# Two layers of a channel-wise likelihood as 32x32 products in differing array tiles

## The chip, the cores and the metric

The kernel runs on one core of one Trainium2 chip. The metric is the device time of one execution in microseconds (us). Before the change the median of three runs was 16118.02 us (16114.57 to 16145.0). A profile holds the engine records and the granted TensorE clock of one execution.

## The reference

A clustered attention and an MLP with a depthwise 3x3 convolution come first. The change lies in what follows, a likelihood for each of 192 channels. Each channel has its own four tiny layers (1 to 3, 3 to 3, 3 to 3, 3 to 1), applied to x - 0.5 and to x + 0.5, which I call the two sides:

```python
def _logits_cumulative(x, Ms, bs, fs):
    for i, (M, b) in enumerate(zip(Ms, bs)):
        x = jnp.einsum('coi,cin->con', jax.nn.softplus(M), x) + b
        if i < len(fs):
            x = x + jnp.tanh(fs[i]) * jnp.tanh(x)
    return x
...
lower = _logits_cumulative(flat - 0.5, Ms, bs, fs)
upper = _logits_cumulative(flat + 0.5, Ms, bs, fs)
s = jax.lax.stop_gradient(-jnp.sign(lower + upper))
pmf = jnp.abs(jax.nn.sigmoid(s * upper) - jax.nn.sigmoid(s * lower))
...
return jnp.maximum(pmf, LIKELIHOOD_BOUND)
```

There are 4 images of 128 x 128 tokens. A block is 512 tokens, so there are 128 blocks, 32 for each image.

## The kernel before

Forty channels make a group, with 3 filters 120 rows; the last of the five groups has 32 channels. A layer of a group is one product with a 120x120 block-diagonal matrix for each side. The convolution's taps are VectorE instructions, and the scheduler puts them between VectorE's instructions for the likelihood of another block.

```python
def bend(g, layer, src):                      # src + gate * tanh(src + bias)
    m = rows_of(g)
    t = pool.tile([R, 2, NB], F32, tag="t", bufs=2, ...)
    for s in range(2):
        nc.scalar.activation(t[:m, s, :], src[:m, s, :], AF.Tanh, bias=bias[:m, layer, g, s:s + 1])
    u = pool.tile([R, 2, NB], F32, tag="u", bufs=6, ...)
    nc.vector.scalar_tensor_tensor(u[:m], t[:m], gate[:m, layer, g:g + 1], src[:m], ALU.mult, ALU.add)
    return u
...
for layer, lw in ((1, l1w), (2, l2w)):
    for g in range(NG):
        m = rows_of(g)
        ps = ps2(f"h{layer}_{n}_{g}")         # one of two PSUM tiles of two banks
        for s in range(2):
            mm(ps[:m, s, :], lhsT=lw[:m, g].rearrange("p c o -> p (c o)")[:, :m],
               rhs=us[g][:m, s, :], start=True, stop=True)
        us[g] = bend(g, layer, ps)
for part, b3t, c0, m, gs in ((l3a, bias3a, 0, CA, (0, 1, 2)), (l3b, bias3b, CA, CB, (3, 4))):
    ps = ps2(f"h3_{n}_{m}")
    ...                                       # layer 3: products l3a, then l3b
    nc.vector.tensor_tensor(lu[:m], lu[:m], sg[:m]...., ALU.mult)
...
# convolve(i): the taps, on VectorE
nc.vector.scalar_tensor_tensor(
    acc[:, k, r0:r1, :], src[:, k, s0:s0 + r1 - r0, dx:dx + W],
    dwt[:, k, t:t + 1], acc[:, k, r0:r1, :], ALU.mult, ALU.add)
...
for i in range(NBLK + 2):
    ...                                       # expand(i): norm, transposes, fc1
    convolve(i - 1)
    likelihood(i - 2)
```

Of the kernel before, what the change touches and what calls it, by code (L numbers as in the profile page):

```python
# [9 lines left out]
F32 = mybir.dt.float32  # L10
# [9 lines left out]
C = 192          # channels  # L20
C1 = C - P       # channels in the second chunk of a contraction
HEADS = 8
D = C // HEADS   # 24
M = 64           # cluster means
MLP = 384
W = 128          # image width: 128 tokens are one image row
NB = 512         # tokens in a block
NJ = NB // P     # token tiles (= image rows) in a block
G = 40           # channels in a group of the last layer
CA = 3 * G       # channels of part a of the last layer, three groups  # L30
CB = C - CA      # channels of part b, two groups
R = 3 * G        # rows (channel, filter) of a group
NG = 5
HR = 32          # rows or columns of a head: 24, and some for its shifts or its sum
# [5 lines left out]
def conv_seq_kernel(  # L40
# [7 lines left out]
    NT = N // P      # token tiles, attention groups, image rows  # L48
# [18 lines left out]
    # ---------------------------------------------------------------- constants  # L67
# [6 lines left out]
    # tri[k, m] = 1 where k < m  # L74
# [9 lines left out]
    # cluster numbers less M, all negative, and each token's own number  # L84
# [7 lines left out]
    # ---------------------------------------------------------------- weights  # L92
    # Contractions over the channels are in two chunks, of 128 and of 64 rows. Where a
    # layer norm comes before, its gain scales the rows, and a 65th row of the second
    # chunk, against ones, holds what its offset contributes.
# [18 lines left out]
    l0a = const([CA, 3, G, 3], "l0a")  # L114
    l0b = const([CB, 2, G, 3], "l0b")
    l1w = const([R, NG, G, 3], "l1w")
    l2w = const([R, NG, G, 3], "l2w")
    l3a = const([R, 3, CA], "l3a")
    l3b = const([R, 2, CB], "l3b")
    gate = const([R, 3, NG], "gate")  # L120
    bias = const([R, 3, NG, 2], "bias")
# [3 lines left out]
    def rows_of(g):  # L125
        return R if g < NG - 1 else 3 * (C - (NG - 1) * G)

    with tc.tile_pool(name="prep", bufs=2) as prep:
# [8 lines left out]
        def norm_params(g, b, name):  # L137
            ga, gb = load(g, 1, f"g_{name}", 1)
            # the offset as a 65th column, so that its product lands on partition 64
# [31 lines left out]
        # A head has 32 rows: 24 of its own, one for each of the two shifts of a query's  # L171
        # scores (against its keys and against the means), and 6 zeros. Keys have a one
        # in the first of the two, the means' keys in the second.
# [4 lines left out]
        # and values a one, for the sum of a query's weights  # L178
# [3 lines left out]
        # the means: unit vectors to compare with, keys and values  # L182
# [53 lines left out]
        # Wproj @ Wconv  # L236
# [17 lines left out]
        # The last layer's matrices: softplus(m) = max(m, 0) + log1p(exp(-|m|)), in columns  # L254
        # by rows (channel, filter) of a group, and by channels for its first layer.
        NS = 8 * NG + 6
        raw = prep.tile([P, NS], F32, bufs=1)
        nc.vector.memset(raw, 0.0)
        rawg = raw[:, 0:8 * NG].rearrange("p (g e) -> p g e", e=8)
        vecs = prep.tile([R, 6, NG], F32, bufs=1)  # L260
        nc.vector.memset(vecs, 0.0)
        m0r = m0.rearrange("c (o u) -> (c o) u", u=1)
        for g in range(NG):
            n = rows_of(g)
            s = slice(g * R, g * R + n)
            nc.sync.dma_start(out=rawg[:n, g, 0:1], in_=m0r[s, :])
            nc.sync.dma_start(out=rawg[:n, g, 1:4], in_=m1[s, :])
            nc.sync.dma_start(out=rawg[:n, g, 4:7], in_=m2[s, :])
            nc.sync.dma_start(out=rawg[:n, g, 7:8], in_=m3[s, :])
            for e, v in enumerate((b0, b1, b2, f0, f1, f2)):  # L270
                nc.sync.dma_start(out=vecs[:n, e, g:g + 1], in_=v[s, :])
        nc.sync.dma_start(out=raw[:CA, 8 * NG:8 * NG + 3], in_=m0[0:CA, :])
        nc.sync.dma_start(out=raw[:CB, 8 * NG + 3:NS], in_=m0[CA:C, :])
        sp = prep.tile([P, NS], F32, bufs=1)
        e1 = prep.tile([P, NS], F32, bufs=1)
        u1 = prep.tile([P, NS], F32, bufs=1)
        c1 = prep.tile([P, NS], F32, bufs=1)
# [3 lines left out]
        # log1p(e) = log(u) + (e - (u - 1)) / u with u the rounded 1 + e  # L281
# [8 lines left out]
        spg = sp[:, 0:8 * NG].rearrange("p (g e) -> p g e", e=8)  # L290
        nc.scalar.activation(gate, vecs[:, 3:6, :], AF.Tanh)

        # rows (c, i) against columns (c', o): one where c = c'
        mask = prep.tile([R, G, 3], F32, bufs=1)
        nc.vector.memset(mask, 1.0)
        nc.gpsimd.affine_select(out=mask, in_=mask, pattern=[[-3, G], [0, 3]], base=0,
                                channel_multiplier=1, compare_op=ALU.is_ge, fill=0.0)
        nc.gpsimd.affine_select(out=mask, in_=mask, pattern=[[3, G], [0, 3]], base=2,
                                channel_multiplier=-1, compare_op=ALU.is_ge, fill=0.0)
# [593 lines left out]
```

## Time and profile before

| | before |
|---|---|
| median of the runs | 16118.02 us |
| span of the profiled execution | 16111.9 us |
| mean granted TensorE clock | 0.883 |
| layers 1 and 2 on TensorE (L786) | 2397.7 us busy |
| one block, mean of 116, from one layer 1 to the next (29 for each image; its last blocks run alone and are shorter) | 63.71 us |

In a row of the costliest groups stand the line, engine and operation, what is written from what, the shapes, the count, the busy time with the mean of one, and the idle time of that engine ahead of it with what ended it. PE stands for TensorE, PEld for its weight loads, DVE for VectorE, ACT for ScalarE and POOL for GpSimd. In a timeline a line has the start, the duration, the engine, the operation and, in brackets, the idle time of the engine ahead of it. The prediction shows these views of the kernel before.

### The profile page before, as it was taken

To read this page: it belongs to the slowest core of one execution; us is meant where nothing else is said; L and a number is where in the kernel's file an instruction comes from. 1 tells how busy PE (TensorE), PEld (TensorE's weight loads), DVE (VectorE), ACT (ScalarE), POOL (GpSimd) and SP (SyncE) were. 2 spreads that over 40 slices of the span, in tenths; PEclk is the share of its full clock that TensorE was granted. 3 is DMA by queue.
4 is the path that set the end of the run, shared out by engine and by line. 5 is a ranking of instruction groups with operands and counts; after the bars stand their busy time and mean duration, and the time that the engine had idled before them with its cause. 6 is when DMAs were issued, how large, how long until landed. Compare 5 with 4: busy or idle time off the path is not lost.

```text
span 16111.9 us, 185400 instructions
## 1 busy us (share of the span) xinstructions
PE 13647.8 (85%) x72162; PEld 7179.5 (45%) x72162; DVE 9317.3 (58%) x16584; ACT 6563.8 (41%) x9595; POOL 3769.5 (23%) x4503
## 2 busy tenths in 40 slices
PE   6669998888877999788887799988888999988888
PEld 5546663333354666333335466533333566533333
DVE  6534446777753444677776344477777344477776
ACT  1023334555512333455551233355555333355555
POOL 1441112222214111222211411122222211122222
PEclk6579998999967999899995899989999999999999
DMA  2100000000020000000002000000000000000000
GB/s 72 58 14 19 17 16 26 19 19 19 13 65 14 19 19 15 26 18 20 19 13 65 16 17 19 18 22 20 19 18 13 19 17 19 22 20 18 20 19 12
DMA packets 297421, 366.60 MB, mean 23 GB/s; under 512 B 56479, under 2 KB 206431, under 8 KB 296543
## 3 DMA queue, kind: packets, MB, share of 16 engines
q1 hardware_dynamic: 231006, 253.71, 5.3%
q0 software_dynamic: 65536, 101.02, 2.4%
q8 instruction: 570, 9.34, 0.2%
q14 instruction: 309, 2.52, 0.1%
HBM read 203.31 MB, written 151.26 MB: 22 GB/s over the span
## 4 chain that ended last, share of the span: by engine, by line
PE 53%; DVE 23%; issue 8%; POOL 7%; ACT 6%; DMA 2%; SPq 0%; POOLq 0%; DVEq 0%; ACTq 0%
DVE acc_f L741 8%; PE st L597 7%; DVE u_f L772 6%; PE h_f L786 4%; PE av L622 4%; PE h_f L794 4%; PE sm L560 4%; DVE mx L561 4%; PE ph_f L718 3%; PE ps_a L522 3%; PE ps_a L523 3%; PE ph_f L719 2%; PE av L625 2%; ACT t_f L770 2%; POOL sg_f L800 2%
## 5 line engine op out<-in xcount | busy, mean ns | idle before, releaser
L770 ACT ACTIVATE t_f<-h_f,bias 120x512 f32<-120x512 f32 (+1 forms) x3840 | 2394.7, 683 | 1714.9 <-PE h_f L786 1313.2
L741 DVE SCALAR_TENSOR_TENSOR acc_f<-hd_f,dwt,acc_f 128x128 f32<-128x128 f32 (+2 forms) x5304 | 2500.3, 517 | 565.0 <-ACT hd_f L720 514.9
L772 DVE SCALAR_TENSOR_TENSOR u_f<-t_f,gate,h_f 120x1024 f32<-120x1024 f32 (+1 forms) x1920 | 2416.0, 1274 | 243.6 <-ACT t_f L770 240.7
L600 ACT ACTIVATE es<-st 128x1024 f32<-128x1024 f32 (+1 forms) x1024 | 1043.1, 1020 | 2387.9 <-PE st L597 2335.2
L597 PE MATMUL st<-qa,kt_a 26*128 26x256 f32 (+1 forms) x8192 | 1163.1, 410 | 364.1 <-DVE mx L561 364.1
L786 PE MATMUL h_f<-u_f,l2w 120*120 120x512 f32 (+1 forms) x2560 | 1204.5, 606 | 247.4 <-DVE u_f L772 247.3
L561 DVE TENSOR_REDUCE mx<-sm 128x4 f32<-128x1024 f32 (+1 forms) x1024 | 1202.4, 1217 | 336.3 <-PE sm L560 193.3
L786 PE MATMUL h_f<-u_f,l1w 120*120 120x512 f32 (+1 forms) x2560 | 1193.2, 605 | 28.6 <-DVE u_f L772 28.6
L688 POOL DMA_INDIRECT at_f<-at_d,pos x512 | 616.9, 1205 | 2149.7 <-PE pb_gf L383 1901.2
L645 POOL TENSOR_TENSOR ot<-on 128x192 f32<-128x192 f32 x512 | 302.9, 592 | 3331.7 <-DVE on L641 3330.2
L597 PEld LDWEIGHTS st<-qa,kt_a 26*128 26x128 f32 x8192 | 707.3, 190 | 814.7 <-DVE mx L561 757.8
L534 DVE COPY va_a<-pv_a 128x512 f32<-128x512 f32 x256 | 177.0, 691 | 1410.2 <-PE pv_a L533 1410.2
L802 DVE TENSOR_TENSOR lu_f<-lu_f,sg_f 120x1024 f32<-120x1024 f32 (+1 forms) x256 | 317.3, 1240 | 1080.8 <-ACT sg_f L801 1080.7
L718 PE MATMUL ph_f<-ta_f,fc 128*128 128x512 f32 x768 | 607.0, 883 | 394.9 <-ACT ta_f L381 394.9
L800 POOL TENSOR_TENSOR sg_f<-lu_f 120x512 f32<-120x512 f32 (+1 forms) x256 | 383.3, 1497 | 2187.0 <-ACT lu_f L798 2177.4
L786 PEld LDWEIGHTS h_f<-u_f,l2w 120*120 120x120 f32 (+1 forms) x2560 | 417.4, 178 | 1011.7 <-DVE u_f L772 627.0
L794 PE MATMUL h_f<-u_f,l3a 120*120 120x512 f32 x1536 | 692.1, 600 | 128.1 <-DVE u_f L772 128.1
L786 PEld LDWEIGHTS h_f<-u_f,l1w 120*120 120x120 f32 (+1 forms) x2560 | 441.4, 180 | 746.5 <-issue 602.2
L622 PE MATMUL av<-es,va_a 128*32 128x128 f32 x16384 | 769.6, 307 | 0.0
L639 DVE RECIPROCAL rec<-ao 128x16 f32<-128x16 f32 x512 | 131.7, 257 | 1098.4 <-PE ao L636 1098.4
L629 ACT COPY sums<-av 128x512 f32<-128x512 f32 x512 | 299.8, 585 | 1110.8 <-PE av L625 1099.8
L579 DVE TENSOR_TENSOR qa<-qt_a,pm 128x256 f32<-128x256 f32 x512 | 215.5, 421 | 894.9 <-PE pm L578 893.0
(291 smaller groups left out, 23682.5 us busy)
## 6 DMA issues: line engine op xcount, KB each, us to landing
xn_d<-xn_c SPq DMA_DIRECT2D x128, 384.0 KB
at_d<-ot SPq DMA_DIRECT2D x128, 384.0 KB
xa_c<-in_x SPq DMA_DIRECT2D x128, 256.0 KB
xa_f<-in_x SPq DMA_DIRECT2D x128, 240.0 KB
out<-pm_f SPq DMA_DIRECT2D x128, 240.0 KB
xb_f<-in_x SPq DMA_DIRECT2D x128, 144.0 KB
out<-pm_f SPq DMA_DIRECT2D x128, 144.0 KB
xb_c<-in_x SPq DMA_DIRECT2D x128, 128.0 KB
```

Of the source, the lines that this page charges most:

```text
L560: mm(psv[:, h, t, 0:n], lhsT=qt[r, t, qs], rhs=kt[r, t, c0:c0 + n], start=True, stop=True)
L561: nc.vector.tensor_reduce(mx[:, :, 2 * a:2 * a + 2, D].rearrange("p t h -> p h t"), psv[:, :, :, 0:n], AX.X, ALU.max)
L597: mm(psv[:, h, t, :], lhsT=kt[r, t, ks], rhs=qa[r, t, q0_:, :].rearrange("p w q -> p (w q)"), start=True, stop=True)
L600: nc.scalar.activation(e[:, :, :, q0_ * P:], psv, AF.Exp)
L622: mm(av[HR * r:HR * r + HR, 0, t, :], lhsT=blocks[k // NJ][2][:, k % NJ, 4 * t + r, :], rhs=es[r // 2][:, r % 2, t, c0:c0 + P], start=w == ...
L718: mm(ps, lhsT=fc1_0[:, s], rhs=ta, start=True, stop=False)
L741: nc.vector.scalar_tensor_tensor(acc[:, k, r0:r1, :], src[:, k, s0:s0 + r1 - r0, dx:dx + W], dwt[:, k, t:t + 1], acc[:, k, r0:r1, :], ALU. ...
L770: nc.scalar.activation(t[:m, s, :], src[:m, s, :], AF.Tanh, bias=bias[:m, layer, g, s:s + 1])
L772: nc.vector.scalar_tensor_tensor(u[:m], t[:m], gate[:m, layer, g:g + 1], src[:m], ALU.mult, ALU.add)
L786: mm(ps[:m, s, :], lhsT=lw[:m, g].rearrange("p c o -> p (c o)")[:, :m], rhs=us[g][:m, s, :], start=True, stop=True)
L794: mm(ps[:m, s, :], lhsT=part[:r, k], rhs=us[g][:r, s, :], start=k == 0, stop=k == len(gs) - 1)
L800: nc.gpsimd.tensor_tensor(sg[:m], lu[:m, 0, :], lu[:m, 1, :], ALU.add)
```

## The change

The intent: in a 120x120 block-diagonal product only one cell in forty does anything. Ten channels (30 rows, padded to 32) are enough for a product of their own, and eight such products (four quarters, two sides) lie in eight different 32x32 tiles of the array, meant to run at the same time. In layer 1 a quarter's output is turned to other rows, by a step that differs with the side, so that the sides' tiles differ as well. As the two sides then have their gates in different rows, layer 1's u_f is made side by side.

```diff
+    def turn(layer, g, s):
+        return 2 * (g % 2) + s if layer == 1 else 0
...
-                    nc.vector.scalar_tensor_tensor(u[:m], t[:m], gate[:m, layer, g:g + 1], src[:m], ALU.mult, ALU.add)
+                    for v in ([slice(0, 1), slice(1, 2)] if layer == 1 else [slice(0, 2)]):
+                        nc.vector.scalar_tensor_tensor(u[:, v], t[:, v], gate[:, layer, g, v.start:v.start + 1],
+                                                       src[:, v], ALU.mult, ALU.add)
...
-                        for s in range(2):
-                            mm(ps[:m, s, :], lhsT=lw[:m, g].rearrange("p c o -> p (c o)")[:, :m],
-                               rhs=us[g][:m, s, :], start=True, stop=True)
+                        for q in range(Q):
+                            for s in range(2):
+                                r = 32 * ((q + turn(layer - 1, g, s)) % Q)
+                                c = 32 * ((q + turn(layer, g, s)) % Q)
+                                w = l1w[r:r + 32, g] if layer == 1 else l2w[r:r + 32, g, s]
+                                mm(ps[c:c + 32, s, :], lhsT=w, rhs=us[g][r:r + 32, s, :], start=True, stop=True)
```

Cut from the diff: the preparation of weights, gates and biases in the new rows, layers 0 and 3 on 128 rows or columns, and comments.

## The prediction

> **What bounds the kernel now.** I read the busy shares and slices first, then the costliest groups, then the timeline of one block, then the busy time of short windows with the granted clock. The page:
>
> ```profile
> PE 13647.8 (85%) x72162; PEld 7179.5 (45%) x72162; DVE 9317.3 (58%) x16584; ACT 6563.8 (41%) x9595; POOL 3769.5 (23%) x4503
> ...
> PEclk6579998999967999899995899989999999999999
> ...
> L770 ACT ACTIVATE t_f<-h_f,bias 120x512 f32<-120x512 f32 (+1 forms) x3840 | 2394.7, 683 | 1714.9 <-PE h_f L786 1313.2
> ...
> L772 DVE SCALAR_TENSOR_TENSOR u_f<-t_f,gate,h_f 120x1024 f32<-120x1024 f32 (+1 forms) x1920 | 2416.0, 1274 | 243.6 <-ACT t_f L770 240.7
> ...
> L786 PE MATMUL h_f<-u_f,l2w 120*120 120x512 f32 (+1 forms) x2560 | 1204.5, 606 | 247.4 <-DVE u_f L772 247.3
> ...
> L786 PE MATMUL h_f<-u_f,l1w 120*120 120x512 f32 (+1 forms) x2560 | 1193.2, 605 | 28.6 <-DVE u_f L772 28.6
> ```
>
> The two L786 rows are what changes: 2397.8 us of TensorE, 15% of the span. PE at 85% suggests a big prize, but that is an average. The MLP and likelihood stage has 4 x 32 = 128 blocks; from 2700 to 4300 us a block takes 63.7 us (mean of 24 starts of the same instruction), half of the whole time. Inside a block, layers 1 and 2 are a ring: TensorE makes h_f in one of two PSUM tiles, ScalarE makes t_f, VectorE makes u_f and so frees the tile. The TensorE and VectorE timelines of layer 2 of one block:
>
> ```profile
> 3313.12 3.71 PE L786 MATMUL h_f<-u_f,l2w 120*120 120x512 f32 x8 [0.94 <-DVE u_f L772]
> 3317.89 3.81 PE L786 MATMUL h_f<-u_f,l2w 120*120 120x512 f32 x8 [1.05 <-DVE u_f L772]
> 3322.77 5.41 PE L794 MATMUL h_f<-u_f,l3a 120*120 120x512 f32 x12 [1.07 <-DVE u_f L772]
> ```
>
> ```profile
> 3314.71 1.93 DVE L741 SCALAR_TENSOR_TENSOR acc_f<-hd_f,dwt,acc_f 128x128 f32<-128x128 f32 x4
> 3316.56 1.27 DVE L772 SCALAR_TENSOR_TENSOR u_f<-t_f,gate,h_f 120x1024 f32<-120x1024 f32 x1
> 3317.75 0.75 DVE L741 SCALAR_TENSOR_TENSOR acc_f<-hd_f,dwt,acc_f 128x512 f32<-128x512 f32 x1
> 3318.41 1.27 DVE L772 SCALAR_TENSOR_TENSOR u_f<-t_f,gate,h_f 120x1024 f32<-120x1024 f32 x1
> 3319.60 1.92 DVE L741 SCALAR_TENSOR_TENSOR acc_f<-hd_f,dwt,acc_f 128x384 f32<-128x384 f32 x3
> ```
>
> TensorE does two groups per 4.8 us and is busy 3.7 of them, but VectorE has almost no holes: its queue fills the ring with convolution taps. Averaged over the 24 blocks, VectorE idles only 0.22, 0.44, 0.28 and three times 0.04 us between the first u_f of layer 0 and the u_f of group 3 in layer 2: 1.05 us of 27.9. So the stretch is **bound by VectorE's queue and the ring at nearly the same length**. VectorE's large holes (7.2 us before the first L802 of a block, 3.7 before the first tap on the new hd_f, 1.5 for the norm) are in the stretches that follow, behind layer 3 and behind the transposes and fc1 products, which the change leaves alone.
>
> [...] L622 (128-row, 32-column tiles, 128 columns streamed, f32) runs 16 records in 0.66 us, in sets of four started 13 to 14 ns apart, one set per 109 ns; one after the other they would take 16 x 107 ns = 1.7 us. The step to the next mode is 203 ns from the last start.
>
> ```profile
> 1523.73 0.66 PE L622 MATMUL av<-es,va_a 128*32 128x128 f32 x16
> 1524.33 0.44 PE L625 MATMUL av<-eg,vgx 128*64 128x128 f32 x4
> ```
>
> [...] Here four row tiles write one bank, in different partitions; no trace of before shows that case. [...] (PEclk column, 1.00 or 0.50):
>
> ```profile
> 3327.76:3331.18 3.42, 3.42 (x9) 1.14 (x8) 0.00 (x0) 1.58 (x3) 1.26 (x1) 1.00 0.00 0
> 3331.18:3334.59 3.41, 1.10 (x10) 0.68 (x7) 2.64 (x9) 3.22 (x4) 0.25 (x2) 1.00 0.00 0
> 3334.59:3338.00 3.41, 1.81 (x8) 1.18 (x8) 1.63 (x4) 0.69 (x2) 3.32 (x3) 0.50 0.00 0
> ...
> 3344.83:3348.24 3.41, 3.41 (x5) 1.33 (x4) 2.09 (x5) 1.31 (x2) 1.37 (x1) 0.50 0.04 11
> 3348.24:3351.65 3.41, 3.41 (x9) 1.48 (x8) 2.42 (x8) 2.64 (x5) 0.00 (x0) 1.00 0.11 32
> ```
>
> [...] After an idle stretch the fc1 products need 4 to 7 us to get full clock back.
>
> **The change, part by part.**
> 1. TensorE, layers 1 and 2. A 120x120 product of 512 columns is two records 429 ns apart; a group has two sides, so 4 x 0.429 = 1.72 us. After, a group is 8 products in 8 different tiles, two per row group and two per column group. If they overlap as L622's do, a group streams 2 x 0.429 us plus 7 x 13.5 ns of starts = 0.95 us. For 10 groups: 17.2 to 9.5 us a block, so 128 x 7.7 = **986 us of TensorE time go**, most of it off the path.
> 2. The ring. Its 4.76 us (load at 3313.12 to load at 3317.88) are: 1.39 to the last record's start, 0.63 until ScalarE starts, 1.42 for the two tanh and hand-over, 1.27 for u_f, 0.05. The first term becomes about 0.63, so the ring 4.0 us for two groups. VectorE needs 9.3 us of work for the four groups of layer 2 that took 9.65, so VectorE becomes the sole bound.
> 3. VectorE. Layer 1's u_f is split by side: 2 x 0.66 for 1.19 us (start to start), +0.13 x 5 = 0.65 us a block. The order listing puts one 0.53 us tap behind group 3 instead of before it. With 0.13 us plus columns/0.96 ns per instruction, which fits the starts in the trace, the work from u_f of layer 0 to group 3 of layer 2 is 26.42 before and 26.54 us after; measured were 27.87. So at most 1.3 us a block, and of the named idle 1.05 - 0.12 = **0.9 us a block, 120 us in all, if the clock stays full**.
> 4. The clock. In layer 2 a row group now streams 0.87 us per group of about 2.3 us, 0.38: [...] I expect half clock by the second half of layer 2. Then a group takes 1.9 us, the ring 5.0, and layer 2 is bound by it: the gain shrinks to about 0.5 us. Then layer 3 starts cold. Its 12 records take 5.15 us on the chain to VectorE's 7.2 us hole; TensorE idles some 1 us before them, [...] **+2.15 us**. Sum with half clock: -0.5 + 2.15 = +1.6 us a block, x 128 = about +200 us.
> 5. Preparation: about 100 small copies more at the start, at some 0.1 to 0.2 us, beside loads: under 20 us. Layers 0 and 3 use 128 rows or columns for 120: free, since time goes by the columns streamed. ScalarE's 683 ns stay.
>
> **The rivals.**
> A. Full clock stays [...]: -120 us, 16000. B. Half clock from layer 2 into layer 3: +200, 16320. C. The tiles don't overlap [...]: 8 products in two waves are as long as before; in four waves a group takes 3.4 us and layers 1 and 2 are bound by TensorE, +15 us a block, far slower. For overlap: L622's four column tiles, and pairs of L597's row tiles starting 6 ns apart. Against: four row tiles in one bank are new. D. TensorE really is the bound, and 986 us come off: against it stand VectorE's full queue, and that of the 276.0 us of idle ahead of these products (247.4 + 28.6), 275.9 ended with VectorE's u_f.
>
> **Range and chances.** A 0.3, B 0.6, C 0.1 (at about +600 as a mean of mild and bad): 0.3 x (-120) + 0.6 x 200 + 0.1 x 600 = +144 us, so 16260. The low end is A with all 1.3 us recovered (-165 gives 15950); the high end is B with 6 us until full clock in every block (3 us lost: +320) and layer 1 partly cold too, 16500. Faster by 2% would need 2.5 us a block, more than VectorE's idle in the stretch: 0.03. Slower by 2% needs +2.5 us a block: B at its worst or C, 0.16.
>
> **What would show it.** Step 1: L786's successor busy near 1200 us for both layers, starts of 8 records within 0.1 us. Steps 2 and 3: VectorE's idle before u_f well under 243.6 us, DVE busy up by about 80 us. Step 4: mean granted clock under 0.883, PEclk below 9 in the slices of this stage, and l3a's 12 records longer than 5.4 us. If the clock stays and the time falls, A; if l3a stays at 5.4 us while the time rises, the half-clock story is wrong. A much longer L786 is C.

The terms of the sum: -0.5 + 2.15, given as +1.6 us a block or about +200 us, and with the chances +144 us, 16260. Two of its steps are estimates. The first is that 0.38 of a window's time (1.30 of 3.41 us) brings half clock; the views show a window at full clock with 1.10 us of work in 3.41 that was followed by half clock, and one at half clock with 3.41 us that was followed by full. The second is the +2.15 us: layer 3a at half clock for 4.3 us in the mean, half of them lost. In the trace of before records of 512 columns that follow each other start 429 ns apart at full clock and 853 ns at half (medians), and in all 120 places where the fc1 products begin anew, full clock came 3.65 to 6.99 us after their first start. For the other estimates of the prediction the same trace has: VectorE's instructions of 128, 384, 512 and 1024 columns, one after the other, start 0.26, 0.53, 0.66 and 1.19 us apart; TensorE's records of 512 columns have a median duration of 592 or 593 ns with 72x120, 120x120 and 128x120 alike (rows x columns); small copies in the preparation (128x64) start 0.13 us apart.

## More of the kernel before

The instruction that multiplies lu_f by its sign runs once a block for the first 120 channels, so the distance between its starts is the time of a block. From VectorE's timeline of the kernel before:

```profile
2694.04 1.23 DVE L802 TENSOR_TENSOR lu_f<-lu_f,sg_f 120x1024 f32<-120x1024 f32 x1 [7.22 <-ACT sg_f L801]
...
2757.89 1.22 DVE L802 TENSOR_TENSOR lu_f<-lu_f,sg_f 120x1024 f32<-120x1024 f32 x1 [7.22 <-ACT sg_f L801]
...
2822.23 1.23 DVE L802 TENSOR_TENSOR lu_f<-lu_f,sg_f 120x1024 f32<-120x1024 f32 x1 [7.22 <-ACT sg_f L801]
...
2885.14 1.23 DVE L802 TENSOR_TENSOR lu_f<-lu_f,sg_f 120x1024 f32<-120x1024 f32 x1 [7.22 <-ACT sg_f L801]
```

The blocks take 63.85, 64.34 and 62.91 us, together 191.10, and then the same three come again. The instructions are the same in each.

## The result, and the profile after

| | before | after |
|---|---|---|
| runs in the same rounds, us | 16112.38 to 16145.0, median 16116.3 | 16156.76, 16181.08, 16200.82, 16230.05; median 16190.95 |
| span of the profiled execution, us | 16111.9 | 16154.7 |
| mean granted clock | 0.883 | 0.845 |

The ratio is 1.0043 (95% interval 1.0025 to 1.0061). A ratio here and below is the mean time of one kernel's fast runs over the mean of the other's in the same rounds, so it is not quite the ratio of the medians quoted. The time is the same within 2%, as expected, but it rose by about half of the 142 us that were predicted. The executions of the changed kernel also spread over 73 us, more than twice as far as before.

The page of the changed kernel: the engines, the granted clock in 40 slices, and the rows of u_f, layer 2, layer 3a and layer 1.

```profile
PE 13107.1 (81%) x87582; PEld 6649.4 (41%) x87582; DVE 9394.2 (58%) x17398; ACT 6553.2 (41%) x9595; POOL 3667.6 (23%) x4495
...
PEclk6579998888867999888885799988888999988888
...
L807 DVE SCALAR_TENSOR_TENSOR u_f<-t_f,gate,h_f 128x1024 f32<-128x1024 f32 (+1 forms) x2560 | 2484.6, 1007 | 129.9 <-ACT t_f L803 120.8
...
L824 PE MATMUL h_f<-u_f,l2w 32*32 32x512 f32 x10240 | 950.3, 809 | 473.0 <-DVE u_f L807 469.0
...
L830 PE MATMUL h_f<-u_f,l3a 128*120 128x512 f32 x1536 | 775.8, 660 | 203.8 <-DVE u_f L807 203.8
...
L824 PE MATMUL h_f<-u_f,l1w 32*32 32x512 f32 x10240 | 616.6, 706 | 130.0 <-DVE u_f L807 124.3
```

Layers 1 and 2 now keep TensorE busy for 950.3 + 616.6 = 1566.9 us instead of 2397.7. VectorE waits half as long ahead of u_f (129.9 for 243.6 us), and its busy time is 77 us higher. Digits of 8 have come into the clock's row, and layer 3a takes 84 us more. Its mean hides what happens. TensorE's timeline has these four blocks in a row:

```profile
3151.31 7.11 PE L830 MATMUL h_f<-u_f,l3a 128*120 128x512 f32 x12 [2.07 <-DVE u_f L807]
...
3215.20 5.41 PE L830 MATMUL h_f<-u_f,l3a 128*120 128x512 f32 x12 [1.30 <-DVE u_f L807]
...
3277.67 7.11 PE L830 MATMUL h_f<-u_f,l3a 128*120 128x512 f32 x12 [2.07 <-DVE u_f L807]
...
3341.57 5.41 PE L830 MATMUL h_f<-u_f,l3a 128*120 128x512 f32 x12 [1.35 <-DVE u_f L807]
```

Layer 3a either has its old duration or is 1.70 us longer. Two stretches say why. They are cut at the edges of the clock's windows, which the trace's clock records place on a fixed grid (3.4133 us in the mean over the trace, and no record off it by more than 0.001). A row gives the stretch, its length, the busy time of PE, PEld, DVE, ACT and POOL with counts, then the granted clock (rounding at the cut makes 0.97 of 1.00 and 0.53 of 0.50). First the end of layer 2 and layer 3a of the block whose products start at 3215.20:

```profile
3203.63:3207.04 3.41, 1.09 (x16) 0.21 (x16) 3.41 (x6) 1.39 (x4) 0.00 (x0) 0.97 0.16 48
3207.04:3210.45 3.41, 2.29 (x24) 0.45 (x32) 3.41 (x7) 2.22 (x4) 0.14 (x1) 0.50 0.00 0
3210.45:3213.87 3.42, 3.42 (x32) 0.23 (x16) 3.35 (x6) 1.48 (x3) 0.00 (x0) 0.53 0.00 0
3213.87:3217.28 3.41, 2.11 (x12) 1.02 (x6) 3.00 (x4) 1.26 (x2) 0.00 (x0) 1.00 0.00 0
```

And of the block whose layer 3a starts at 3277.67:

```profile
3271.89:3275.31 3.42, 1.89 (x32) 0.37 (x32) 3.38 (x5) 2.41 (x4) 0.00 (x0) 1.00 0.00 0
3275.31:3278.72 3.41, 1.34 (x10) 0.47 (x3) 3.38 (x5) 1.26 (x2) 0.00 (x0) 0.97 0.01 2
3278.72:3282.13 3.41, 3.41 (x6) 1.38 (x5) 0.62 (x1) 0.00 (x0) 0.00 (x0) 0.53 0.00 0
3282.13:3285.55 3.42, 3.42 (x10) 1.33 (x9) 0.00 (x0) 0.73 (x2) 0.00 (x0) 1.00 0.00 0
```

In both a thin window (1.09 and 1.34 us of work) is followed by half clock. But at half clock the small products stream nearly twice as long (16 records of a group in 1.96 us instead of 1.09), fill a window (3.42 us in the first block), and full clock is back. In the first block this happens inside layer 2, before layer 3a. In the second the thin window ends one microsecond after layer 3a has begun. Whether layer 3a is hit thus depends on where the grid falls.

I then measured, in every block, the time from the last window edge to the first product of layer 1 (the phase), and the time to the next block's first product. "Half in 1" is how much of layer 1 ran at half clock. The changed kernel's 116 blocks:

| phase, us | blocks | time of the block | half in 1 | from layer 1's start to layer 3a | layer 3a, first to last start |
|---|---|---|---|---|---|
| 2.80 to 3.00 | 31 | 62.01 | 0 | 25.84 | 4.82 |
| mostly 3.00 to 3.38 | 23 | 63.50 | 0.7 | 26.1 | 4.82 |
| 3.38 to 3.56 (0.15 past an edge) | 29 | 64.28 | 3.41 | 26.13 | 6.51 |
| 1.67 to 1.72 | 13 | 65.07 | 6.83 | 27.64 | 4.82 |
| mostly 1.88 to 1.96 | 20 | 65.98 | 6.5 | 27.9 | 6.51 |

In the kernel before, layer 1's start to layer 3a is 26.85 us in 108 of 116 blocks and layer 3a is 4.82 us at every phase, and only the stretch from layer 3 over the norm to the next block depends on it. So a block's phase gives its time, its time gives the next block's phase, and the blocks run into repeating patterns. Before it is 62.91 + 63.87 + 64.36 = 191.14 us, which is 56 windows (56 x 3.4133 = 191.147). After it is either 62.00 + 64.28 (37 windows, 63.1 us a block), in 60 blocks, or chiefly 63.5 + 65.07 + 65.98 (57 windows, 64.85 us a block), in the other 56, whose mean is 64.75. **Half of the changed kernel's blocks are 0.6 us faster than before, the other half 1.0 us slower.**

The profiled execution adds up: +22 us in these 116 blocks, +10 in the last blocks of the images (layer 3a and layer 1 at half clock there as well), +11 up to the first layer 1 (preparation), together the 43 us by which the span grew. It was the fastest of the four executions (16156.76 us). That the slower ones (up to 16230 us) had more blocks in the slow pattern is an inference: they have no profile of their own. If the 60 fast blocks of the profiled execution were slow as well, it would take 60 x 1.64 = 98 us more, some 16255, an estimate from these numbers; the runs lie below that.

### The profile page after: what moved, and what is told of

It reads as the page before. It is cut to its first block, busy times and chain, and to the rows that moved or that the text cites. A ratio compares the mean times of both kernels' runs of the same rounds, so it can differ in the third digit from the quotient of the medians.

```text
span 16154.7 us, 217985 instructions
## 1 busy us (share of the span) xinstructions
PE 13107.1 (81%) x87582; PEld 6649.4 (41%) x87582; DVE 9394.2 (58%) x17398; ACT 6553.2 (41%) x9595; POOL 3667.6 (23%) x4495
## 5 line engine op out<-in xcount | busy, mean ns | idle before, releaser
L803 ACT ACTIVATE t_f<-h_f,bias 128x512 f32<-128x512 f32 x3840 | 2382.2, 685 | 1632.5 <-PE h_f L824 971.0
L807 DVE SCALAR_TENSOR_TENSOR u_f<-t_f,gate,h_f 128x1024 f32<-128x1024 f32 (+1 forms) x2560 | 2484.6, 1007 | 129.9 <-ACT t_f L803 120.8
L824 PE MATMUL h_f<-u_f,l2w 32*32 32x512 f32 x10240 | 950.3, 809 | 473.0 <-DVE u_f L807 469.0
L722 POOL DMA_INDIRECT at_f<-at_d,pos x512 | 520.6, 1017 | 1918.3 <-PE pb_gf L417 1707.8
L830 PE MATMUL h_f<-u_f,l3a 128*120 128x512 f32 x1536 | 775.8, 660 | 203.8 <-DVE u_f L807 203.8
L824 PE MATMUL h_f<-u_f,l1w 32*32 32x512 f32 x10240 | 616.6, 706 | 130.0 <-DVE u_f L807 124.3
L594 PE MATMUL sm<-kt_a,qt_a 24*128 24x256 f32 x8192 | 711.2, 405 | 8.6 <-issue 6.9
L790 PE MATMUL py_f<-acc_f,fc 128*120 128x512 f32 (+1 forms) x1536 | 682.8, 593 | 0.0
```

The source lines that it names most:

```text
L594: mm(psv[:, h, t, 0:n], lhsT=qt[r, t, qs], rhs=kt[r, t, c0:c0 + n], start=True, stop=True)
L790: mm(ps[:m], lhsT=fc2[:, k, s], rhs=acc[:, k].rearrange("p r w -> p (r w)"), start=k == 0, stop=k == 2)
L803: nc.scalar.activation(t[:, s, :], src[:, s, :], AF.Tanh, bias=bias[:, layer, g, s:s + 1])
L807: nc.vector.scalar_tensor_tensor(u[:, v], t[:, v], gate[:, layer, g, v.start:v.start + 1], src[:, v], ALU.mult, ALU.add)
L824: mm(ps[c:c + 32, s, :], lhsT=w, rhs=us[g][r:r + 32, s, :], start=True, stop=True)
L830: mm(ps[:m, s, :], lhsT=part[:, k], rhs=us[g][:, s, :], start=k == 0, stop=k == len(gs) - 1)
```

## The experiments

A first theory was the prediction's own: layer 2 at half clock costs layer 3 its clock, and what VectorE gains is given back there. The rival was that TensorE's time or the split u_f sets the result. The theory of patterns came out of these runs' surprises. There were 18 runs with 5 rounds each (two kernels have 4 results), each against the kernel before on the same chip.

| run | median, us | ratio to before (95%) | us a block* |
|---|---|---|---|
| again (the changed kernel) | 16176.68 | 1.0042 (1.0029 to 1.0056) | 63.93 |
| fill2 | 16488.1 | 1.0230 (1.0216 to 1.0244) | 66.5 |
| fill12 | 16608.62 | 1.0305 (1.0291 to 1.0319) | 67.1 |
| shared | 16079.59 | 0.9977 (0.9963 to 0.9990) | 63.35 |
| l2full | 16248.87 | 1.0082 (1.0068 to 1.0095) | 64.83 |
| l12full | 16144.06 | 1.0019 (1.0005 to 1.0032) | 63.74 |
| before_warm | 17173.14 | 1.0659 (1.0644 to 1.0674) | 72.6 |
| shared_warm | 17269.5 | 1.0716 (1.0702 to 1.0731) | 73.4 |
| after_tick | 16169.4 | 1.0031 (1.0017 to 1.0044) | 63.90 |
| before_tick | 16065.11 | 0.9967 (0.9953 to 0.9980) | 63.19 |
| after_cut | 16129.29 | 1.0005 (0.9991 to 1.0019) | 63.62 |
| shared_warm2 | 16089.99 | 0.9980 (0.9967 to 0.9994) | 63.12 |
| before_cut | 16052.03 | 0.9962 (0.9949 to 0.9976) | 63.26 |
| before_d96 | 16139.92 | 1.0017 (1.0003 to 1.0030) | 63.90 |
| after_d96 | 16336.95 | 1.0135 (1.0119 to 1.0151) | 65.9 |
| shared_late | 15816.51 | 0.9816 (0.9803 to 0.9830) | 60.36 |
| before_late | 15827.0 | 0.9817 (0.9804 to 0.9831) | 60.66 |
| shared_late4 | 15913.59 | 0.9871 (0.9856 to 0.9886) | 61.27 |

*Mean of 112 blocks in the profiled execution, by the starts of the lu_f instruction, the first 28 distances of each image (63.69 before; 63.89 for the changed kernel's first profile). The profile of after_d96 is of its slowest execution (16396.72 us).

### again: the changed kernel once more

> The changed kernel again, as the yardstick of this call. Both theories: 16156 to 16230 us, as in its four runs, 1.002 to 1.007 of before; layer 3a's twelve records from first to last start 4.82 us where the clock is full and 5.7 to 6.9 us in the blocks where it is half, half clock in about 40% of the blocks there.

The second profile shows the same two patterns and the same five block times within 0.05 us, and layer 3a again at half clock in 47 of 112 steady blocks. The effect is not an accident of one execution.

### shared: both sides of a quarter in one tile

```diff
-        return 2 * (g % 2) + s if layer == 1 else 0
+        return 2 * (g % 2) if layer == 1 else 0
...
-                    for v in ([slice(0, 1), slice(1, 2)] if layer == 1 else [slice(0, 2)]):
+                    for v in [slice(0, 2)]:
```

> The 32x32 products, but both sides of a quarter in the same array tile, so four tiles at a time and twice 0.86 us a group, 1.72 us as the 120x120 products took; layer 1's u_f in one instruction again. Theory clock: row groups stream 1.72 us a group again, the clock stays full from layer 0 to layer 3, layer 3a 4.82 us, and the time is that of before within 0.3%, 16070 to 16160 us. Rival tiles (the 32x32 mode itself, its changes of mode and its four times as many instructions cost the time): 0.3 to 0.5% slower than before, like the changed kernel, with the clock full.

Four tiles run at a time, a group takes about as long on TensorE as before the change (1.94 us for its 16 records, 1.88 for the four records before), and u_f is whole. Layer 3a took 4.82 us in every block, layer 2 never lost the clock, and the kernel is 0.2% faster than before. Smaller products with the old streaming time did no harm here. The blocks alternate between 62.6 and 63.7 us (37 windows in two), with a slip to 64.5 every nine blocks or so.

### fill2 and fill12: more work on TensorE in the changed kernel

```diff
                         ps = ps2(f"h{layer}_{n}_{g}")
+                        for _ in range(1 if layer == 2 else 0):
+                            mm(ps[:, 0, :], lhsT=ident, rhs=us[g][:, 0, :], start=True, stop=True)
```

fill12 has the condition `layer == 2 or g >= 2`.

> The changed kernel with one more 128x128 product of 512 columns ahead of each of layer 2's five groups, into the same PSUM tile, overwritten by the group's own products: 0.86 us more TensorE work a group, 128 x 5 x 0.86 = 550 us in all. Theory clock (what the smaller products save is given back because TensorE is too idle to keep its full clock): layer 2 at full clock in nearly all blocks, layer 3a at 4.82 us in nearly all blocks (mean of the changed kernel 5.55), the layer 2 stretch of VectorE at most 0.4 us longer, so 0.3 to 0.7 us a block less, 40 to 90 us faster than the changed kernel in spite of 550 us more work. Rival VectorE (the stretch is bound by VectorE's queue and the clock is beside the point): no gain, 0 to 50 us slower than the changed kernel, layer 3a unchanged.

> As fill2, and one more such product ahead of layer 1's groups 2, 3 and 4. Theory clock: full clock in layers 1 and 2 in nearly all blocks; VectorE's waits from the first u_f to layer 2 fall from a mean of 0.74 us to below 0.4 us a block, layer 3a at 4.82 us: 1.0 us a block, about 120 us faster than the changed kernel, near 16070 us and thus below before. Rival VectorE: as long as the changed kernel or slower, since 8 x 0.86 us more TensorE work a block only delays the ring.

As expected, layer 2 and layer 3a ran at full clock in all blocks (layer 3a 4.82 us). Yet both runs were slower, because layer 1 was then at half clock in 109 of 112 blocks of fill2, for 8.8 us a block in the mean. Both also moved convolution taps in VectorE's order (fill12 waits 2.4 us a block in layer 2), so their size tells nothing. What fill2 does show is a pattern: 65.55 + 67.57 = 133.12 us, 39 windows, held all through an image.

### l2full and l12full: the small products undone, the rest of the change kept

```diff
-    l2w = const([P, NG, 2, 32], "l2w")
+    l2w = const([P, NG, 2, P], "l2w")       # the four 32x32 matrices in their places, zeros elsewhere
...
+                        if layer == 2:       # l12full: both layers
+                            for s in range(2):
+                                mm(ps[:, s, :], lhsT=l2w[:, g, s], rhs=us[g][:, s, :], start=True, stop=True)
```

> The changed kernel with one part undone: layer 2 is again one product of 128 rows and 128 columns per side (the four quarters of a group on the diagonal, in their turned places), layer 1 stays as 32x32 products in differing tiles, and layer 1's u_f stays split by side. VectorE's order in the stretch of layers 1 and 2 is the same as in the changed kernel. Theory (the clock: layer 2's small products leave too little work in TensorE's windows, so that layer 3 starts at half clock in about 40% of the blocks): layer 2 and layer 3a run at full clock in every block, layer 3a's twelve records take 4.82 us from first start to last instead of 5.55, and nothing else moves; -0.73 us a block, about -90 us against the changed kernel, so about 16095 us, ratio to before about 0.9985. TensorE's work goes up by about 500 us against the changed kernel and the time still falls. Rival (TensorE's time in layer 2 counts): the time rises above 16250. Rival (the loss is in the split u_f and VectorE's order, not in the clock): the time stays at 16180 to 16200.

> The changed kernel with layers 1 and 2 both as one product of 128 rows and 128 columns per side, on the new layout of rows, with layer 1's u_f still split by side: all of the change but the small products. This is the cost of the split and of the layout alone, at full clock. Theory (the stretch is bound by VectorE's queue with little idle time in it): VectorE's extra 0.65 us a block shows nearly whole in the stretch from the first u_f of layer 0 to layer 2, less what it fills of the idle 0.94 us there, so +0.3 to +0.65 us a block, +40 to +80 us against before: 16155 to 16200, ratio 1.0025 to 1.005; full clock in layers 1, 2 and 3a in all blocks. Rival (the split lets TensorE and ScalarE start a side earlier and is free): ratio 0.999 to 1.001.

l12full costs 0.2%, half of the changed kernel's loss: the price of the split u_f and the new rows at full clock, with layer 1's taps in another order. Its blocks keep to before's pattern of three in 56 windows. l2full is a miss. Layer 3a was at 4.82 us in every block, as expected, but the time rose. VectorE's order was also not quite the same, contrary to what I wrote: two taps had changed places with a u_f in layer 2. From VectorE's timeline of l2full:

```profile
3483.68 1.22 DVE L850 TENSOR_TENSOR lu_f<-lu_f,sg_f 120x1024 f32<-120x1024 f32 x1 [6.44 <-ACT sg_f L849]
...
3548.53 1.23 DVE L850 TENSOR_TENSOR lu_f<-lu_f,sg_f 120x1024 f32<-120x1024 f32 x1 [6.44 <-ACT sg_f L849]
```

Nearly every block takes 64.85 us, 19 windows (64.853). Having repaired layer 3a, the kernel has settled at the phase 2.18 us, at which layer 1 runs at half clock for 6.8 us (108 of 112 blocks have more than 3.5 us of it) and takes 2 us longer. Five blocks took 63.3 us instead, with 1.4 us of layer 1 at half clock in the mean. This run suggested that phases, not the work alone, set the time.

### before_warm, shared_warm and shared_warm2: products that nobody reads, against the half clock around the norm

> The kernel before with the same six products that nobody reads in a block, around the norm's hole. Theory: as for the version that shares tiles, -1 to -2 us a block, ratio 0.984 to 0.992, granted clock well over 0.883. It shows what half clock costs on a chain that VectorE waits for. Rival: the added products stand in the way, ratio 1.0 to 1.01.

> The version in which both sides of a quarter share a tile (four tiles at a time, u_f whole, 16080 us), with three products of 512 columns that nobody reads put on TensorE after layer 3b and three more before the fc1 products, so that its clock does not fall in the hole around the norm. Theory: VectorE's 3.7 us wait for the first hd_f in each block is half caused by the fc1 products at half clock; with full clock there they come 1 to 2 us earlier, so -1 to -2 us a block, -130 to -260 us: 15820 to 15950, ratio 0.981 to 0.990. Rival (the waits around the norm are set by VectorE, ScalarE and the transposes, and the added products themselves stand in the way of the transposes, 1.3 us): no gain or a loss, ratio 0.997 to 1.01.

Both lost 9 to 10 us a block, by a fault of mine. The added products read lu_f, which was only final after the sigmoid, so TensorE's queue stood still ahead of the transposes until then (in before_warm no product ran from 3364.13 to 3370.96 us): a new wait. shared_warm2 has as operand a u_f that is there already:

```diff
+            for _ in range(3):
+                mm(pa, lhsT=ident[:idle.shape[0]], rhs=idle, start=True, stop=True)    # idle: u_f of group 3, layer 2
...
+                    if k == 0:
+                        mm(ps, lhsT=ident, rhs=xn.rearrange("p j c -> p (j c)")[:, 0:NB], start=True, stop=True)
```

> The version in which both sides of a quarter share a tile, with three products nobody reads after layer 3b's transposes (this time their operand is an old u_f, there before layer 3 begins, so that they wait for nothing) and one more between the transposes of xn: the repair of the run that kept the clock up and lost 1060 us because its added products waited for the end of the block's sigmoid. Theory: the fc1 products then run at full clock and VectorE's first hd_f comes 1 to 2 us earlier in most blocks: 15820 to 15990, ratio 0.981 to 0.992. Rival: the added products delay the transposes of xn by more than the clock gives: ratio 0.998 to 1.01.

The granted clock rose to 0.903, and the half clock between the lu_f instruction and the next block's first u_f fell from 10.7 (shared) to 5.1 us a block, but the time did not move (0.9980 against 0.9977 for shared). The scheduler's order changed too, so I can't say what each part is worth. The blocks kept to a pattern of 62.58 + 63.71 us, 37 windows, as in shared. The expected -1 to -2 us a block was wrong.

### after_tick and before_tick: one copy of one element more

```diff
+                        if (layer, g) == (2, 1):
+                            nc.vector.tensor_copy(tick, us[g][0:1, 0, 0:1])
```

> The changed kernel with one VectorE instruction more in a block, a copy of a single element after u_f of group 1 of layer 2, some 0.1 us by the starts of the shortest VectorE instructions in the trace (0.09 us apart); the order is otherwise the same on every engine. New theory: the clock's windows run free at 3.413 us, the time of a block depends only on where in a window the block begins, and the blocks run into repeating patterns whose sum is a whole number of windows: the changed kernel spends part of its blocks in a pattern of two (62.00 + 64.28 us, 37 windows, faster than before) and part in one of three (63.5 + 65.07 + 65.98 us, 57 windows, slower). A small delay pushes the phase out of the pattern of two. Iterating the measured table from phase to block time with 0.08 to 0.13 us more gives 64.4 to 64.6 us a block instead of 63.9, so +65 to +90 us: 16245 to 16270 for 13 us of added work. Rival (block times just add up): +0.1 us a block, +13 us, 16190 to 16195.

> The kernel before with the same one-element copy. New theory: before sits in a pattern of three (62.91 + 63.87 + 64.36 us, 56 windows) that takes up small delays by shifting its phase (slopes of -0.5 us of block time per us of phase), up to about 0.04 us a block; with 0.08 to 0.13 us it is pushed past an edge: iterating the table gives 63.9 to 64.6 us a block instead of 63.7, +20 to +115 us, with two thirds of the phases never visited before, so this size is a rough one; the repeating pattern again adds up to a whole number of windows. Rival (block times add up): +0.1 us a block, +13 us, every block longer by the same amount.

These expectations are wrong in their premise. I had compared only part of the order. In before_tick one tap of 384 columns moved behind the last u_f that layer 3a needs, in after_tick two taps moved behind one more u_f: from the first u_f of layer 2 to the end of group 3's, the stretch became 0.24 us shorter in the first (8.96 for 9.20 us) and 0.5 in the second. What remains is that the size of the work and the time don't go together: 0.24 us less on the path gave 0.5 us a block in before_tick, 0.5 less gave nothing in after_tick (16169.4 against 16176.68 for again, measured on another chip call).

### after_cut: 33 ns less in the changed kernel

```diff
+                            e = W - 8 if (k, t) == (2, 5) else W
                             nc.vector.scalar_tensor_tensor(
-                                acc[:, k, r0:r1, :], src[:, k, s0:s0 + r1 - r0, dx:dx + W],
-                                dwt[:, k, t:t + 1], acc[:, k, r0:r1, :], ALU.mult, ALU.add)
+                                acc[:, k, r0:r1, :e], src[:, k, s0:s0 + r1 - r0, dx:dx + e],
+                                dwt[:, k, t:t + 1], acc[:, k, r0:r1, :e], ALU.mult, ALU.add)
```

> The changed kernel with one convolution tap of a block eight columns short in each image row (480 columns instead of 512; its result is wrong on purpose), in the stretch of layer 2: 33 ns of VectorE work less in a block, order unchanged. New theory: the phase now drifts back out of the pattern of three and stays longer in the pattern of two; iterating the table with -0.033 us gives 63.57 us a block instead of 63.9: -35 to -45 us, about 16135 to 16150. Rival (block times add up): -4 us, 16170 to 16185.

The order on VectorE is the same but for one swap at the start of each of the four images, TensorE's is the same altogether; the result is wrong on purpose (the comparison with the reference still passed). 33 ns of VectorE's work less, 4 us in all, took the time from 16176.68 (again) to 16129.29 us, 0.37% by the ratios. That is what the table of phases said in advance, and eleven times what adding up says. Of its 116 blocks 69 were at 61.97 or 64.28 us, for 60 of the changed kernel.

### before_cut: 0.2 us less in the kernel before

The same edit with `W - 48`, in the kernel before, with the order kept as well as in after_cut.

> The kernel before with one convolution tap of a block, between the u_f of groups 1 and 2 of layer 2, cut from 512 to 320 columns (its result is wrong on purpose): 0.2 us of VectorE's work less on the path; the order on all engines is the same. Theory (patterns of whole windows): before's pattern of three blocks in 56 windows (63.716 us a block) can't hold with 0.14 us or more less; it falls into a pattern of two blocks in 37 windows, of about 62.7 and 63.6 us: 63.147 us a block, -0.57 us, 116 such blocks: -66 us, about 16050, ratio about 0.9960. Rival (block times add up): -0.1 to -0.2 us a block, -12 to -25 us, 16094 to 16107, ratio 0.9985 to 0.9992, with three block times as in before, each shorter by the cut.

16052.03 us, ratio 0.9962: the expectation was 16050 and 0.9960, and 0.9985 or more if block times add up. The cut was 0.20 us (9.00 for 9.20 us in layer 2). From VectorE's timeline of before_cut, the same instruction as above:

```profile
2881.31 1.23 DVE L803 TENSOR_TENSOR lu_f<-lu_f,sg_f 120x1024 f32<-120x1024 f32 x1 [7.14 <-ACT sg_f L802]
...
2945.03 1.23 DVE L803 TENSOR_TENSOR lu_f<-lu_f,sg_f 120x1024 f32<-120x1024 f32 x1 [7.14 <-ACT sg_f L802]
...
3007.72 1.23 DVE L803 TENSOR_TENSOR lu_f<-lu_f,sg_f 120x1024 f32<-120x1024 f32 x1 [7.14 <-ACT sg_f L802]
...
3071.34 1.23 DVE L803 TENSOR_TENSOR lu_f<-lu_f,sg_f 120x1024 f32<-120x1024 f32 x1 [7.14 <-ACT sg_f L802]
```

63.72, 62.69, 63.62: the pattern of three blocks in 56 windows has become one of two in 37, as expected. The block of 64.36 us is gone but for a slip (64.2 to 64.4 us) in 8 of 112 blocks, so that the mean in the table is 63.26 us and not the 63.147 of the pattern alone.

### before_d96 and after_d96: a delay ahead of layer 3a

```diff
                     ps = ps2(f"h3_{n}_{m}")
+                    if m == CA:
+                        mm(ps[:m, 0, 0:96], lhsT=part[:, 0], rhs=us[0][:, 0, 0:96], start=True, stop=True)
```

The order on all engines is the same but for this product.

> The kernel before with one product of 96 columns more ahead of layer 3a (overwritten by it), 0.08 us on the chain from u_f to the next block at full clock; the order is otherwise the same on all engines. Theory: the pattern of three blocks in 56 windows takes it up: the phases move by +0.1 to +0.25 us, where the second and third block of the pattern are shorter by half the shift; 63.72 to 63.74 us a block as before, 0 to +3 us (if the first block's phase goes past about 1.75 us, it slips now and then, which costs 1.8 us each time). Rival (block times add up): each of the three block times +0.08, 63.80, +10 us.

> The changed kernel with the same product of 96 columns ahead of layer 3a (0.08 us at full clock, 0.16 at half). Theory: the delay pushes the blocks out of the fast pattern of two; iterating the table from phase to block time gives 64.3 us a block instead of 63.9 (a fifth of the phases not seen before): +35 to +55 us, 16215 to 16235. Rival (block times add up): +0.08 to +0.12 us a block, +10 to +15 us, 16188 to 16195.

The delay was not 0.08 us but 0.21 (layer 3a from first to last start 5.03 for 4.82 us). In the kernel before it cost 25 us, 0.21 us a block: the pattern of three couldn't take it up, and a longer one came, with blocks of 63.1 to 64.6 us. Here the mean is just what adding up gives for 0.21 us, so the expectation of no change was not borne out, and it wasn't tested at 0.08. In the changed kernel the same product cost 160 us against again (two chip calls apart, by the ratios 0.93%), six times as much. From VectorE's timeline of after_d96:

```profile
3231.59 1.23 DVE L840 TENSOR_TENSOR lu_f<-lu_f,sg_f 120x1024 f32<-120x1024 f32 x1 [9.25 <-ACT sg_f L839]
...
3297.09 1.23 DVE L840 TENSOR_TENSOR lu_f<-lu_f,sg_f 120x1024 f32<-120x1024 f32 x1 [7.30 <-ACT sg_f L839]
...
3364.72 1.23 DVE L840 TENSOR_TENSOR lu_f<-lu_f,sg_f 120x1024 f32<-120x1024 f32 x1 [9.24 <-ACT sg_f L839]
...
3430.22 1.23 DVE L840 TENSOR_TENSOR lu_f<-lu_f,sg_f 120x1024 f32<-120x1024 f32 x1 [7.30 <-ACT sg_f L839]
```

65.50 + 67.63 us are 39 windows (133.12). The bracket is VectorE's hole behind layer 3: 9.25 us where layer 3a met half clock, 7.30 where it didn't. The fast pattern of two is gone altogether. The direction was expected; the size (35 to 55 us) was not, for a delay over twice as long and phases not seen before.

### shared_late, before_late and shared_late4: taps moved into VectorE's hole

The holes in these brackets, and before_tick's moved tap, seemed to point to another lever: taps that run in the stretch that VectorE bounds could run in the hole behind it. Their weights are made to depend on a u_f, which keeps the scheduler from placing them earlier:

```diff
+            held_taps = [(2, 7), (2, 8)]          # shared_late4: (2, 5) to (2, 8), and us[2]
...
+                held = pool.tile([P, 9], F32, tag="held", ...)
+                nc.vector.scalar_tensor_tensor(held, us[3][:, 0, 0:9], 0.0, dwt[:, 2, :], ALU.mult, ALU.add)
...
+                    held = likelihood(i - 2)
+                    if i <= NBLK:
+                        finish(i - 1, held)       # the held taps with weights from held, then gelu
```

> The version in which both sides of a quarter share a tile (16080 us), with the last two taps of the convolution (two pieces of 384 and two of 128 columns, 1.6 us of VectorE) held until u_f of group 3 of layer 2 is there, so that they run in VectorE's 7.2 us hole behind layer 3 instead of inside the stretch that it bounds. Theory (VectorE's queue bounds that stretch): the stretch shrinks by 1 to 1.6 us until the ring binds, 61.4 to 62.3 us a block: 15860 to 15965, ratio 0.984 to 0.991. Rival (the ring of PSUM tiles already binds): less than 0.5 us a block, 16020 to 16080.

> The kernel before, 120x120 products and all, with the last two taps of the convolution held until u_f of group 3 of layer 2 is there (as in shared_late; one small copy of weights more). Theory (VectorE's queue is the bound, not TensorE): nearly the whole gain comes from the taps: 60.4 to 61.5 us a block instead of 63.7, 15840 to 15890, ratio 0.983 to 0.986, within 80 us of shared_late. Rival (the room that the small products give on TensorE is needed for it): 15950 or more, ratio over 0.990.

> The version with shared tiles and four taps held back (512, and three times 384 and 128 columns: 2.9 us) until u_f of group 2 of layer 2 is there. Layer 2 already leaves VectorE idle for 1.74 us a block in shared_late, so it is bound by the ring there; the stretch of layers 0 and 1 can still shrink by up to 0.8 us, and the pattern of 53 windows in 3 blocks would give way to one of 17.5 or fewer windows a block: 59.0 to 60.3 us, 15650 to 15810, ratio 0.971 to 0.981. Rival (the held taps now delay the hole's own work): as shared_late or slower, 15810 to 15900.

shared_late is 1.8% faster than before, more than expected; VectorE's hole behind layer 3 shrank from 7.2 to 5.8 us. before_late, with its 120x120 products, reaches the same ratio (0.9817). So the smaller products contribute nothing to it that the runs resolve. These two are the fastest correct versions, and beat both kernels by far. But the stretch that the taps left hardly shrank. In the mean of the 112 steady blocks, the time from the first u_f of layer 0 to the end of group 3's u_f of layer 2 went from 29.06 us (before) to 28.73 (before_late), and from 28.97 (shared) to 28.62 (shared_late): VectorE has 1.8 us less work there and waits instead, in layer 2 of before_late 1.72 us for 0.11. That is the rival of shared_late's expectation (the ring already binds: less than 0.5 us). The other 2.87 us (2.80 in shared_late) came between the lu_f instruction and the next block's first u_f, where VectorE's work is the same within 0.12 us. ScalarE's timelines of before and of before_late show a reason; each pair of lines is from one block:

```profile
3276.23 0.63 ACT L801 ACTIVATE sg_f<-sg_f 72x512 f32<-72x512 f32 x1 [5.04 <-POOL sg_f L800]
3276.76 0.56 ACT L381 COPY ta_f<-pa_f 128x512 f32<-128x512 f32 x1
```

```profile
3240.90 0.61 ACT L815 ACTIVATE sg_f<-sg_f 72x512 f32<-72x512 f32 x1
3243.82 0.58 ACT L381 COPY ta_f<-pa_f 128x512 f32<-128x512 f32 x1 [2.31 <-PE pa_f L380]
```

In before, ScalarE stands still for the sign of the last 72 channels, whose sum GpSimd makes late, and only then copies the transposed norm (ta_f), 2.92 us after its transposes are done. In before_late GpSimd makes that sum earlier, and ScalarE copies ta_f as soon as it is there: 6.52 us after the lu_f instruction for 9.34, and the first hd_f follows 10.98 us after it for 13.77, in 108 of the 112 steady blocks. shared and shared_late show the same. The scheduler changed this order along with the taps. No run changes it alone, so that it makes most of the gain is read from the traces and not tested. Two starts of the instruction in VectorE's timeline of before_late, four blocks apart:

```profile
3115.14 1.23 DVE L816 TENSOR_TENSOR lu_f<-lu_f,sg_f 120x1024 f32<-120x1024 f32 x1 [5.56 <-ACT sg_f L815]
...
3357.48 1.22 DVE L816 TENSOR_TENSOR lu_f<-lu_f,sg_f 120x1024 f32<-120x1024 f32 x1 [5.56 <-ACT sg_f L815]
```

The four blocks (60.95, 61.20, 59.72 and 60.47 us) take 242.34 us, 71 windows (242.35); shared_late does three in 53. shared_late4 held more taps back, and was slower: it settled at 61.44 us, 18 windows, at a phase where part of layer 1 is at half clock (3.1 us a block). Less work in the stretch, and a worse lock.

## Why the prediction was right or wrong

**Step 1, the overlap, held.** Eight records start 6 to 11 ns apart at full clock, and a group's other eight follow 0.45 us after them. Its last record thus starts 0.50 us after its first (about 0.63 predicted), and in layer 2 the first tanh starts 1.20 us after it, for 2.00 before. In layer 1 the records of two groups even lie between each other, 32 in 1.23 us. Rival C is out: in this run the products of four row tiles, which write different partitions of one PSUM tile, overlapped (the starts 6 to 11 ns apart named above), and the results are correct. The 986 us were computed at full clock. As much of it now runs at half clock, layers 1 and 2 fell by 831 us, and TensorE's busy time by 541 us in all.

**Steps 2 and 3, VectorE as the sole bound, held.** Where layers 1 and 3a had full clock, layer 1's start to layer 3a fell from 26.85 to 25.84 us: -1.0, for the named -0.9. That the ring is nearly as long as VectorE's queue in the kernel before is borne out by before_late: 1.8 us of VectorE's work less, and a stretch only 0.33 us shorter. VectorE's busy time rose by 77 us, for about 80. Rival D is out: layers 1 and 2 lost a third of their TensorE time and no gain of that size came; l12full, which restores it, is faster than the changed kernel.

**Step 4 failed above all in one term, "+2.15 us" for layer 3a.** The mechanism is there: layer 2 was at half clock for 3.4 to 6.7 us in each of the 112 steady blocks. But layer 3a took +1.70 us in 49 of 116 blocks and +0.00 in the others, +0.72 in the mean, a third of the predicted term. With that in its place the prediction's sum of +1.65 us a block becomes +0.2, and +0.19 was measured on these blocks. The rest of the sum differs as well and nearly cancels: from layer 1's start to layer 3a the gain was 0.35 us instead of 0.5 (1.0 where layer 1 kept its clock, but a loss of 0.8 to 1.0 in the 33 blocks with about 6.5 us of layer 1 at half clock, which the prediction had only at its high end), and the rest of the block, over the norm to the next layer 1, got 0.17 us shorter, as other phases meet the half clock there differently; the prediction left that out. The reason given for the 0.5 was wrong too. At half clock the ring (5.0 us for two groups) was to bind layer 2. But from its first u_f to the end of group 3's, layer 2 took 9.13 us in the 47 steady blocks in which it had half clock for 6.8 us and layer 1 none, and 9.20 us before. What was lost was lost in layer 1, so that the 0.35 comes near the 0.5 by luck.

The premise behind the term was "Then layer 3 starts cold". It came from layer 2's streaming share at full clock, 0.38, taken as if it held on. At half clock the same products streamed nearly twice as long (1.96 us a group for 1.09). The windows show 3.42 us of 3.41, and full clock was back for layer 3a in 67 of 116 blocks. The prediction took a mean over all phases, 4.3 us at half clock, the author's estimate. But the phases are not spread evenly: a block's time sets the next one's phase, and the kernel keeps to a few of them. As it happens, the slow pattern alone (64.75 against 63.71 us, +1.04 x 128 = +133 us, an estimate) is what the prediction described, and the fast one (-0.6) is about its rival A. Both occur in one execution.

**What is shown and what is not.** That block times follow the phase and add up to whole windows is read from the traces. That small amounts of work change the time by much more than themselves, by moving the phase, was foretold and measured in after_cut and before_cut with the order kept, and seen in after_d96 with a wrong size. Not shown: why an execution falls into one pattern or the other at the start of an image, what a delay under 0.2 us does to the kernel before, and, by a run of its own, what makes the versions with held taps fast.

**Step 5 held:** the first layer 1 starts 11 us later, and 19 us later in again (under 20). The range (15950 to 16500) held the result, and the class with the chance 0.81 came.

## What to carry to other kernels

Where TensorE works in bursts, price a thinner burst at both clocks: here the same products filled a window at half clock (3.42 us of 3.41), full clock came back, and layer 3a's loss was a matter of phase (49 of 116 blocks) and not of every iteration. Look at the time of each iteration, not only at the mean, and see whether a few of them add up to a whole number of clock windows; then small changes need not show at their size (here 33 ns a block showed as eleven times that, and half a microsecond as nothing), and a comparison of two variants by their totals alone says little about the edit. Relieving an engine that is merely busy can be worth nothing (541 us of TensorE here, and no gain). And where a variant gains more than its reason can give, compare the stretches of a block one by one: here taps taken out of VectorE's full stretch took 0.3 us off it, since the ring was nearly as long, while 2.8 us came where the scheduler had changed the order in which ScalarE got its work.
